# Gate rows and gated biases of the experts as single-pass products of 32 rows, issued at the end of a piece

## The chip, the cores and the metric

The kernel runs on one core of one Trainium2 chip. A core has a TensorE (matrix products into PSUM), a VectorE, a ScalarE, a GpSimd and a SyncE that issues the DMAs; in the profile they are PE (with PEld for its weight loads), DVE, ACT, POOL and SP. The metric is the device time of one execution in microseconds; the median of the runs counts.

## The reference

The input x is 8 images of 256 channels and 32 x 32 points. Layer 0 is a convolution and attention block. Layer 1 takes the 1024 points of an image as tokens t of 256 channels, adds a causal attention of the normalised tokens, and then adds a mixture of eight experts. Cut to what matters here:

```python
def ffn(x, Wr, br, W1, ..., W2, ..., Wo, bo):      # x: normalised tokens (b, f, d)
    feat = mean(x, axis=0)                         # over the images
    w = softmax(feat @ Wr + br, axis=-1)           # (f, e): one gate per token place and expert
    h = relu(bn(einsum('bfd,edh->bfeh', x, W1) + b1))
    h = relu(bn(einsum('bfeh,ehk->bfek', h, W2) + b2))
    y = einsum('bfeh,ehd->bfed', h, Wo) + bo
    return einsum('bfed,fe->bfd', y, w)
```

All eight experts are computed for every token; the gate only weights them. The gate depends on the place f and the expert e, not on the image. So the weighted biases, the sum over e of w[f,e] * bo[e], are the same for all images too.

## The kernel before

The kernel works in three parts. Layer 0 (to about 1421 us) and the attention of layer 1 (to about 2085 us) are untouched but for their tail. The third part, the experts, runs from about 2090 us to the end.

**Gates.** The function `gate(h)` handles one half h of the 1024 places. TensorE forms the logits lg (matmuls with feat as weights), VectorE and ScalarE make a softmax in `ge` (128 places x 4 tiles x 8 experts), four transposes turn it into PSUM (`pwT`, 8 x 512), and VectorE copies it to `wT` (8 experts x 1024 places, f32). `gate(0)` runs in the last stretch of the attention, ahead of the layer norm of the last half; `gate(1)` is the last work before the experts.

**Visits and pieces.** The experts are taken in two groups G of four. A visit is (G, half h, image b), 32 in all, in the order G, then h, then b; each has four slots s, one per expert: 128 pieces. Piece n starts layer 1 (W1) of its own expert, while layer 2 (W2) works on piece n-2 and layer 3 (Wo) on piece n-4. In the loop over n, four rounds i = 0..3 advance the three layers as generators and then do the VectorE and ScalarE steps that were put off from the piece before (`soon`). The engines are driven through `InOrder`, which keeps the program's order on each of them, so what is written first is queued first.

**Precision.** Most expert products are F32R, in one pass, of 12-bit upper and lower parts (`products`); layer 2 of the even experts is plain f32 (`pm<-h,w`). The gate rows and the gated biases are plain f32.

**Gate rows.** `gate_rows(G, h, s)` spreads the gate of one expert over all 128 partitions: a product of `sel8` (8 x 8 x 128, ones where row and expert agree) with `wT`, into `pw`, and a ScalarE copy to `wb`. Layer 2 multiplies by it (`gated`) three pieces later. It is needed only for the first image of a (G, h), so at 16 pieces: 0 to 3, 32 to 35, 64 to 67 and 96 to 99. `gated_bias(h, g)` does the same with `boT` (the expert biases, transposed on TensorE through `pbo`), into `pg` and then `gb`, for pieces 0, 1, 32 and 33. `gb` is added to the tokens `te` at slot 2. Both are issued at the head of the piece, before layer 1.

**Buffers.** PSUM has eight banks: one each for the two outputs of layer 1 (`pa`), two for `pm`, `pw`, `pg` and `pbo` together (pool `ps_b`), and four for layer 3 (`q`). Two products in a row for the same bank have to wait for whoever reads it.

**Queues.** SyncE issues all DMAs in order. At the opening of the experts it issues the remaining weights, the tokens `te` and the parts `ze` of the next visits, about 10 MB.

**Opening.** The tiles of the experts (pool `hp`) take over memory of the attention's pools, so the first instruction of each engine on such a tile waits until the attention's last users are done. `sel8` is made there by GpSimd (a memset, line 1626, and an affine select, line 1627).

The calls in the loop, which the change moves:

```python
if b == 0:
    gate_rows(G, h, s)
    if G == 0 and s < KC:
        gated_bias(h, s)
```

Of the kernel before, what the change touches and what calls it, by code (L numbers as in the profile page):

```python
# [9 lines left out]
F32 = mybir.dt.float32  # L10
F32R = mybir.dt.float32r
AF = mybir.ActivationFunctionType
ALU = mybir.AluOpType
# [4 lines left out]
P = 128  # L18
B, C, H, W = 8, 256, 32, 32
N = H * W  # L20
HALF = 512
KC = C // P
NH, KD, HD = 4, 32, 64
HID = 2 * C
NE = 8
# [79 lines left out]
def conv_attn_hybrid_kernel(  # L105
# [22 lines left out]
    nc = tc.nc  # L128
# [11 lines left out]
    def col(name, i=0, n=1):  # L140
        o, w = _VOFF[name]
        assert i + n <= w
        if o >= NVEC0:
            return more[0][:, o - NVEC0 + i : o - NVEC0 + i + n]
        return vec[:, o + i : o + i + n]

    def cols(name):
        return col(name, 0, _VOFF[name][1])

    ident = const.tile([P, P], F32, name="ident")  # L150
# [323 lines left out]
    pe, dve = InOrder(tc, nc.tensor, TensorCost()), InOrder(tc, nc.vector, vector_cost)  # L474
    act, pool = InOrder(tc, nc.scalar), InOrder(tc, nc.gpsimd)
    t = [None] * B
    with ExitStack() as l0:
        wpool = l0.enter_context(tc.tile_pool(name="w0", bufs=1))
        one = l0.enter_context(tc.tile_pool(name="one0", bufs=1))
# [27 lines left out]
        sel = one.tile([nf, P], F32, tag="full", name="sel", bufs=2)  # L507
# [60 lines left out]
        for half in range(2):  # L568
            nc.gpsimd.affine_select(
                out=pickr, in_=pickr, compare_op=ALU.not_equal, fill=1.0, base=-NH * half,  # L570
                pattern=[[-1, NH], [0, HD]], channel_multiplier=1,
# [7 lines left out]
        for half in range(2):  # L579
            nc.gpsimd.affine_select(  # L580
                out=pickn, in_=pickn, compare_op=ALU.not_equal, fill=1.0, base=-nq * half,
                pattern=[[-1, nq]], channel_multiplier=1,
# [444 lines left out]
        def gate(b):  # L1027
            hid = hid_of[b]
            while len(hid["out"]) < hid["gelu"] and ng + len(hid["out"]) in hid["h"]:
                g = len(hid["out"])  # L1030

                prod = two.tile([P, N], F32, tag="hid", name="hid", bufs=ng + 1)
                blocks = prod.rearrange("p (n k r c) -> p k n r c", r=PS, k=2, c=W // 2)
                a, b2 = (hid["h"][j].rearrange("p (n r k c) -> p k n r c", r=PS, k=2, c=W // 2) for j in (g, ng + g))
                for k in range(2):
                    dve.tensor_mul(blocks[:, k], a[:, k], b2[:, k])
                hid["out"].append(prod)
                if hid["alone"]:
                    mix(b, g)
# [189 lines left out]
    wm = ctx.enter_context(tc.tile_pool(name="wm", bufs=1))  # L1229
# [3 lines left out]
    nc.sync.dma_start(wrs, wr.rearrange("(k p) e -> p k e", p=P))  # L1233
    brs = wm.tile([1, NE], F32, name="brs")
    nc.sync.dma_start(brs, br)
    wT = wm.tile([NE, N], F32, name="wT")

    NG, SLOTS = 2, NE // 2
    w_d = [[dram.tile([P, 3, KC, C], F32, tag=f"wd{e}_{l}", name=f"wd{e}_{l}") for l in range(3)] for e in range(NE)]
# [2 lines left out]
    def in_parts(e, l):  # L1242

        return l != 1 or e % 2 == 1

    def load_expert(pool_, e, l):

        tag = f"w{e % SLOTS}_{l}"
        if not in_parts(e, l):
            w_ = pool_.tile([P, KC, C], F32, tag=tag, name=tag, bufs=1)  # L1250
            nc.sync.dma_start(w_, w2[e].rearrange("(k p) o -> p k o", p=P))
        else:
            w_ = pool_.tile([P, 3, KC, C], F32R, tag=tag, name=tag, bufs=1)
            nc.sync.dma_start(w_.bitcast(F32), w_d[e][l])
        w_in[e, l] = w_

    def upper(dst, src, eng=None, positive=False):

        if eng is None:
            act.activation(dst[:, 0], src, AF.Relu if positive else AF.Copy, scale=DOWN)  # L1260
        else:
            eng.tensor_scalar_mul(dst[:, 0], src, DOWN)
# [13 lines left out]
    with ExitStack() as l1:  # L1276
        wpool = l1.enter_context(tc.tile_pool(name="w1", bufs=1))
        one = l1.enter_context(tc.tile_pool(name="one1", bufs=1))
# [3 lines left out]
        ps_t = l1.enter_context(tc.tile_pool(name="ps_t1", bufs=2, space=PSUM))  # L1282
# [10 lines left out]
        def load_w(name, src):  # L1293
# [12 lines left out]
            out=lower, in_=lower, compare_op=ALU.is_ge, fill=0.0, base=0, pattern=[[-1, P]], channel_multiplier=1,  # L1306
# [225 lines left out]
        def gate(h):  # L1532

            nt = NT // 2
            lg = ps_m.tile([P, nt, NE], F32, tag="mm", name="lg")
            for i in range(nt):
                c0 = (h * nt + i) * P
                for k in range(KC):
                    pe.matmul(lg[:, i, :], feat[:, k, c0 : c0 + P], wrs[:, k, :], start=(k == 0), stop=False)
                pe.matmul(lg[:, i, :], ones[0:1, :], brs, start=False, stop=True)  # L1540
            yield 2.0
            ge = one.tile([P, nt, NE], F32, tag="ge", name="ge")
            gs = one.tile([P, nt], F32, tag="gs", name="gs")
            dve.tensor_reduce(gs, lg, AX.X, ALU.max)
            dve.tensor_sub(ge, lg, gs.unsqueeze(2).to_broadcast([P, nt, NE]))
            act.activation(ge, ge, AF.Exp)
            yield 1.0
            dve.tensor_reduce(gs, ge, AX.X, ALU.add)
            dve.reciprocal(gs, gs)
            dve.tensor_mul(ge, ge, gs.unsqueeze(2).to_broadcast([P, nt, NE]))  # L1550
            yield 1.0
            pwT = ps_t.tile([NE, HALF], F32, tag="tp", name="pwT")
            for i in range(nt):
                pe.transpose(pwT[:, i * P : (i + 1) * P], ge[:, i, :], ident)
            dve.tensor_copy(wT[:, h * HALF : (h + 1) * HALF], pwT)
            yield 0.5

# [51 lines left out]
    with ExitStack() as l2:  # L1609
        hp = l2.enter_context(tc.tile_pool(name="hp", bufs=2))  # L1610
        ps_a = l2.enter_context(tc.tile_pool(name="ps_a2", bufs=2, space=PSUM))
        ps_b = l2.enter_context(tc.tile_pool(name="ps_b2", bufs=2, space=PSUM))
# [9 lines left out]
        s2b = const.tile([P, KC * NE], F32, name="s2b")  # L1622
        nc.vector.tensor_scalar_mul(s2b, s2, -1.0 / STEP)

        sel8 = hp.tile([NE, NE, P], F32, name="sel8", bufs=1)
        nc.gpsimd.memset(sel8, 0.0)
        nc.gpsimd.affine_select(
            out=sel8,
            in_=sel8,
            compare_op=ALU.not_equal,  # L1630
            fill=1.0,
            base=0,
            pattern=[[-1, NE], [0, P]],
            channel_multiplier=1,
        )

        boT = hp.tile([NE, KC, P], F32, name="boT", bufs=1)
        bo_g = cols("bo").rearrange("p (e g) -> p g e", g=KC)
        pb = ps_b.tile([NE, KC, P], F32, tag="pm", name="pbo")
        for g in range(KC):  # L1640
            pe.transpose(pb[:, g, :], bo_g[:, g, :], ident)
        dve.tensor_copy(boT, pb)

        visits = [(G, h, b) for G in range(NG) for h in range(2) for b in range(B)]
        pieces = [(v, s) for v in range(len(visits)) for s in range(SLOTS)]
        ts, gate_of, bias_of, h1_of, h2_of, acc_of = {}, {}, {}, {}, {}, {}

        def cut(h):
            return slice(h * HALF, (h + 1) * HALF)
# [13 lines left out]
        def gate_rows(G, h, s):  # L1663

            wb = gate_of[G, h, s] = hp.tile([P, HALF], F32, tag=f"wb{s}", name=f"wb{s}", bufs=1)
            pw = ps_b.tile([P, HALF], F32, tag="pm", name="pw")
            pe.matmul(pw, sel8[:, G * SLOTS + s, :], wT[:, cut(h)], start=True, stop=True)
            act.copy(wb, pw)

        def gated_bias(h, g):  # L1670

            if g == 0:
                bias_of[h] = hp.tile([P, KC, HALF], F32, tag="gb", name="gb", bufs=1)
            pw = ps_b.tile([P, HALF], F32, tag="pm", name="pg")
            pe.matmul(pw, boT[:, g, :], wT[:, cut(h)], start=True, stop=True)
            act.copy(bias_of[h][:, g, :], pw)
# [77 lines left out]
        def layer3(v, s):  # L1754
# [8 lines left out]
            for both in (False, True):  # L1763
                for g in range(KC):
# [12 lines left out]
                    yield  # L1777

        load_expert(hp, 1, 1)
        fetch_t(0)  # L1780
        for s in range(1, SLOTS):
# [5 lines left out]
        for n in range(len(pieces) + LAG3):  # L1787
            one_ = two_ = three = iter(())
            if n < len(pieces):
                v, s = pieces[n]  # L1790
                G, h, b = visits[v]
                if b == 0:
                    gate_rows(G, h, s)
                    if G == 0 and s < KC:
                        gated_bias(h, s)
                if s == 1:
                    fetch_t(v + 1)
                    if v >= 1:
                        fetch_z(v + 1)
                if s == 2 and G == 0:  # L1800
                    dve.tensor_add(ts[v], ts[v], bias_of[h])
                one_ = layer1(v, s)
            if 0 <= n - LAG2 < len(pieces):
                two_ = layer2(*pieces[n - LAG2])
            if n >= LAG3:
                three = layer3(*pieces[n - LAG3])

            now, soon = soon, [[] for _ in range(4)]
            for i in range(4):
                for stage in (one_, two_, three):  # L1810
                    next(stage, None)
                for step in now[i]:
                    step()
            for l, lag in enumerate((0, LAG2, LAG3)):
                if 0 <= n - lag < len(pieces):
                    v, s = pieces[n - lag]
                    if visits[v] == (0, 1, B - 1):
                        load_expert(wm if s == 0 or (s, l) == (1, 0) else hp, SLOTS + s, l)
# [114 lines left out]
```

## Time and profile before

| what | value |
|---|---|
| median of 3 runs | 3236.74 us (3234.16 to 3243.24) |
| the profiled execution | 3235.5 us, of which its span is 3233.8 us |
| TensorE busy | 2962.3 us, 92% of the span |
| VectorE, ScalarE, GpSimd busy | 2385.1, 1569.5, 337.9 us |
| mean granted TensorE clock | 0.964 |

The span is from the first to the last instruction. Busy time of TensorE counts matmuls whose ends are modelled. "PE pw" names the engine and the tile written; `pw<-wT,sel` names what is written and what is read, and the shapes after it give the partitions and elements. An arrow in brackets names what ended the idle time before an instruction. Nearly all instructions carry line 72, the helper that records them, so they are told apart by their tiles.

### The profile page before, as it was taken

The page shows a single profiled execution, that of the slowest core. Times are in us where ns is not written, and L with a number is a line of the kernel's source. Part 1 is how long each engine was busy: PE and PEld are TensorE (multiplying, and loading weights), DVE is VectorE, ACT ScalarE, POOL GpSimd, SP SyncE. Part 2 cuts the span into 40 slices and gives each one's busy share as a digit, 9 for nine tenths or more (in the row PEclk, how much of TensorE's full clock was granted, in tenths as well). Part 3 has the DMA queues.
Part 4 walks back from the last instruction along what each step waited for, and adds up shares of the span by engine and source line. Part 5 has one row for each costly group of instructions (what it writes and reads, how often), then busy time and mean ns, then how long its engine had stood idle before and what let it go on. Part 6 is the DMA issues. An engine that isn't in the chain of part 4 may idle for free.

```text
span 3233.8 us, 41619 instructions
## 1 busy us (share of the span) xinstructions
PE 2962.3 (92%) x16822; PEld 1941.5 (60%) x16822; DVE 2385.1 (74%) x3002; ACT 1569.5 (49%) x2312; POOL 337.9 (10%) x410
## 2 busy tenths in 40 slices
PE   5998899989898999859999999799999999999998
PEld 3654545454555555435666555577767777777776
DVE  1378778777877878655666655488878888887887
ACT  1554455545445445313333333266656666666665
POOL 1121111121212110001122222100000000000000
PEclk9999999999999999989999999799999999999999
DMA  4203030303030300011323311322211242221220
GB/s 149 62 19 79 27 79 27 79 27 79 27 79 27 79 14 8 17 71 69 142 112 118 124 79 52 136 111 86 78 66 66 92 139 103 91 72 65 84 80 26
DMA packets 60061, 237.46 MB, mean 73 GB/s; under 512 B 5382, under 2 KB 13654, under 8 KB 50774
## 3 DMA queue, kind: packets, MB, share of 16 engines
q1 hardware_dynamic: 59862, 234.74, 21.5%
q8 instruction: 134, 2.20, 0.3%
q14 instruction: 65, 0.53, 0.0%
HBM read 143.23 MB, written 91.49 MB: 73 GB/s over the span
## 4 chain that ended last, share of the span: by engine, by line
PE 45%; DVE 7%; ACT 2%; issue 1%; POOL 1%; DMA 0%; SPq 0%; POOLq 0%; ACTq 0%; DVEq 0%
PE pm L72 12%; PE pa L72 11%; PE q L72 11%; PE s L72 4%; PE po L72 3%; PE pv L72 2%; DVE nm L72 1%; DVE pr L72 1%; PE pk L72 1%; DVE parts L72 1%; DVE zt L72 1%; ACT pr L72 1%; DVE st L72 1%; PE tpt L72 1%; PE pw L72 1%
## 5 line engine op out<-in xcount | busy, mean ns | idle before, releaser
L72 PE MATMUL q<-h2p,w 128*128 128x512 f32 x1536 | 485.9, 425 | 2.9 <-DVE h2p L72 1.7
L72 PE MATMUL pa<-ze,w 128*128 128x512 f32 x1488 | 422.5, 392 | 0.0
L72 PEld LDWEIGHTS q<-h2p,w 128*128 128x128 f32 x1536 | 288.9, 188 | 118.2 <-issue 60.4
L72 DVE SCALAR_TENSOR_TENSOR x<-hpad,vec,x 128x1024 f32<-128x1024 f32 x248 | 317.1, 1283 | 39.9 <-ACT x L72 32.8
L72 DVE SCALAR_TENSOR_TENSOR conv<-hpad,vec,conv 128x1024 f32<-128x1024 f32 x256 | 329.3, 1293 | 13.8 <-ACT conv L72 7.2
L72 PEld LDWEIGHTS pa<-ze,w 128*128 128x128 f32 x1488 | 278.9, 188 | 69.8 <-issue 9.5
L72 ACT ACTIVATE h<-pa,bn_o,s1a 128x512 f32<-128x512 f32 x256 | 198.8, 777 | 203.4 <-PE pa L72 203.3
L72 ACT ACTIVATE pT<-s 128x1024 f32<-128x1024 f32 x256 | 247.4, 1024 | 69.1 <-PE s L72 69.1
L72 DVE SCALAR_TENSOR_TENSOR h<-pa,s1b,h 128x512 f32<-128x512 f32 x256 | 191.6, 749 | 113.2 <-PE pa L72 100.8
L72 PE MATMUL po<-pT,vT 128*32 128x256 f32 x4096 | 272.1, 383 | 0.0
L72 PE MATMUL ph<-xn,piw 128*128 128x512 f32 x512 | 244.4, 615 | 3.1 <-DVE xn L72 1.6
L72 PE MATMUL s<-kk,z 128*128 128x512 f32 x512 | 245.2, 609 | 0.9 <-DVE pr L72 0.9
L72 PE MATMUL pm<-h,w 128*128 128x512 f32 x512 | 242.0, 595 | 0.0
L72 PE MATMUL pm<-h1p,w 128*128 128x512 f32 x768 | 216.1, 389 | 0.5 <-DVE h1p L72 0.5
L72 DVE SCALAR_TENSOR_TENSOR o<-vpad,pe_w,o 128x1024 f32<-128x1024 f32 x128 | 163.5, 1282 | 45.2 <-ACT o L72 42.0
L72 PE MATMUL s<-qst,kst 128*128 128x256 f32 x1024 | 175.2, 313 | 14.2 <-DMA kst<-part 12.9
L72 ACT ACTIVATE hpad<-ph,pi_o 128x512 f32<-128x512 f32 x126 | 86.9, 690 | 182.4 <-PE ph L72 182.4
L72 ACT ACTIVATE h2p<-h 128x1024 fp32r<-128x1024 f32 x128 | 134.9, 1054 | 77.8 <-DVE h L72 77.8
L72 PEld LDWEIGHTS po<-pT,vT 128*32 128x32 f32 x4096 | 120.2, 110 | 84.5 <-issue 1.9
L72 PEld LDWEIGHTS s<-qst,kst 128*128 128x128 f32 x1024 | 136.8, 192 | 47.5 <-issue 42.4
L72 PEld LDWEIGHTS pm<-h1p,w 128*128 128x128 f32 x768 | 144.1, 188 | 31.5 <-DVE h1p L72 0.9
L72 PE MATMUL pz<-pow__116,hid 128*128 128x256 f32 x512 | 138.2, 426 | 27.1 <-DVE hid L72 27.1
(241 smaller groups left out, 4811.7 us busy)
## 6 DMA issues: line engine op xcount, KB each, us to landing
ze<-zd SPq DMA_DIRECT2D x31, 1536.0 KB, 6.3
zd<-parts SPq DMA_DIRECT2D x16, 1536.0 KB, 5.5
qst<-part SPq DMA_DIRECT2D x32, 512.0 KB, 8.5
kst<-part SPq DMA_DIRECT2D x32, 512.0 KB, 15.2
te<-ud SPq DMA_DIRECT2D x32, 512.0 KB, 3.9
wd<-parts_w SPq DMA_DIRECT2D x20, 768.0 KB, 3.6
w<-wd SPq DMA_DIRECT2D x20, 768.0 KB, 5.9
t<-in_x_dram SPq DMA_DIRECT2D x8, 1024.0 KB, 4.9
```

Of the source, the lines that this page charges most:

```text
L72: return self._tc.keep_in_program_order(method(*args, **kwargs))
```

## The change

The products of the gate rows and of the gated biases become F32R products over 32 rows: four parts times eight experts. A helper `stacked` splits its source in an upper part (a cast to F32R) and the rest, and lays four copies of the parts side by side in a given order. For the gates the order is upper, lower, upper, lower (`ge4`), for the biases upper, upper, lower, lower (`bo4`), so that the sum over 32 rows holds all four products of parts. For the gate rows `sel8` picks the first two parts alone (ones in rows e and 8 + e). The transposes give 32 rows in place of 8. `sel8` is built in another tile `sel`, which shares the place of `h1p`, by a memset and two selects, and cast by a fourth GpSimd instruction. Last, the calls move from the head of a piece to its end: after the four rounds, before the loads of the next group.

```diff
-    wT = wm.tile([NE, N], F32, name="wT")
+    wT = wm.tile([4 * NE, N], F32R, name="wT")
...
+    def stacked(dst, src, order):
+
+        first = [order.index(i) for i in range(2)]
+        dve.tensor_copy(dst[:, :, first[0]].bitcast(F32R), src)
+        dve.tensor_sub(dst[:, :, first[1]].bitcast(F32R), src, dst[:, :, first[0]])
+        for i, part in enumerate(order):
+            if i not in first:
+                dve.tensor_copy(dst[:, :, i], dst[:, :, first[part]])
...
+            ge4 = one.tile([P, nt, 4, NE], F32, tag="ge4", name="ge4")
+            stacked(ge4, ge, (0, 1, 0, 1))
             yield 1.0
-            pwT = ps_t.tile([NE, HALF], F32, tag="tp", name="pwT")
+            pwT = ps_t.tile([4 * NE, HALF], F32, tag="tp", name="pwT")
             for i in range(nt):
-                pe.transpose(pwT[:, i * P : (i + 1) * P], ge[:, i, :], ident)
+                pe.transpose(pwT[:, i * P : (i + 1) * P], ge4[:, i].rearrange("p a e -> p (a e)"), ident)
...
-        sel8 = hp.tile([NE, NE, P], F32, name="sel8", bufs=1)
-        nc.gpsimd.memset(sel8, 0.0)
-        nc.gpsimd.affine_select(
-            out=sel8,
-            in_=sel8,
...
+        sel8 = hp.tile([4 * NE, NE, P], F32R, name="sel8", bufs=1)
+        sel = hp.tile([4 * NE, NE, P], F32, tag="h1p", name="sel", bufs=1)
+        nc.gpsimd.memset(sel, 0.0)
+        for part in range(2):
+            nc.gpsimd.affine_select(
+                out=sel,
+                in_=sel,
...
+                base=-NE * part,
...
+        nc.gpsimd.tensor_copy(sel8, sel)
...
-        boT = hp.tile([NE, KC, P], F32, name="boT", bufs=1)
-        bo_g = cols("bo").rearrange("p (e g) -> p g e", g=KC)
-        pb = ps_b.tile([NE, KC, P], F32, tag="pm", name="pbo")
+        boT = hp.tile([4 * NE, KC, P], F32R, name="boT", bufs=1)
+        bo4 = hp.tile([P, KC, 4, NE], F32, name="bo4", bufs=1)
+        stacked(bo4, cols("bo").rearrange("p (e g) -> p g e", g=KC), (0, 0, 1, 1))
+        pb = ps_b.tile([4 * NE, KC, P], F32, tag="pm", name="pbo")
         for g in range(KC):
-            pe.transpose(pb[:, g, :], bo_g[:, g, :], ident)
+            pe.transpose(pb[:, g, :], bo4[:, g].rearrange("p a e -> p (a e)"), ident)
         dve.tensor_copy(boT, pb)
...
-                if b == 0:
-                    gate_rows(G, h, s)
-                    if G == 0 and s < KC:
-                        gated_bias(h, s)
...
+            if n < len(pieces) and b == 0:
+                gate_rows(G, h, s)
+                if G == 0 and s < KC:
+                    gated_bias(h, s)
```

## The prediction, made before the changed kernel was run

> **What bounds the kernel now.** I read the page first: busy shares and the costliest groups. TensorE is busy 92% of a span of 3233.8 us, against 74% for VectorE. The changed lines all lie after about 2070 us, where the experts run. Two groups of the page, and two of the by-form list for the products that the change rewrites:
>
> ```profile
> L72 PE MATMUL pa<-ze,w 128*128 128x512 f32 x1488 | 422.5, 392 | 0.0
> L72 PE MATMUL pm<-h1p,w 128*128 128x512 f32 x768 | 216.1, 389 | 0.5 <-DVE h1p L72 0.5
> L72 PE MATMUL pw<-wT,sel 8*128 8x512 f32 x32 | 18.9, 671 | 1.9 <-POOL sel L1627 1.9
> L72 PE MATMUL pg<-wT,boT 8*128 8x512 f32 x8 | 5.5, 766 | 0.7 <-ACT wb L72 0.7
> ```
>
> The last column is idle time before the group: next to none, so in the expert stage TensorE is the bound and time taken off it counts in full. The windows say the same, 240.00 us busy of 240.00 from 2680 to 2920. A gate row (pw) is 16 products in 32 records: two records each, so more than one pass.
>
> Second, the PE timeline at a gate row (first three lines) and at a boundary of pieces without one (last three); columns are start, length, instruction.
>
> ```profile
> 2645.93 0.61 PE L72 MATMUL q<-h2p,w 128*128 128x512 f32 x2
> 2646.47 1.12 PE L72 MATMUL pw<-wT,sel 8*128 8x512 f32 x2
> 2648.56 1.02 PE L72 MATMUL pm<-h,w 128*128 128x512 f32 x2
> ...
> 2129.89 0.62 PE L72 MATMUL q<-h2p,w 128*128 128x512 f32 x2
> 2130.35 1.09 PE L72 MATMUL pa<-ze,w 128*128 128x512 f32 x4
> 2131.28 1.07 PE L72 MATMUL pm<-h1p,w 128*128 128x512 f32 x4
> ```
>
> From q to pm is 2.63 us with the row and 1.39 us without (both hold two q and four pa): a row costs 1.24 us.
>
> Third, the chain of waits where the stage opens.
>
> ```profile
> 2089.54 1.02 PE pwT L72 x4
> 2090.69 0.92 POOL sel L1626
> 2091.65 1.14 POOLq L1929
> 2092.84 2.07 PE pw L72 x2
> 2094.91 1.71 PE pg L72 x2
> 2096.62 2.86 PE pa L72 x6
> 2099.49 2.31 PE pa L72 x6
> 2101.80 1.05 PE pw L72 x2
> ```
>
> The first row waits for GpSimd to build sel8, and runs at half clock (2.07 against 1.05 us): TensorE is at 0.50 until about 2101.0 by short windows. The first real work, pa, starts at 2096.6.
>
> Fourth, piece 32, the first of half 1, in the PE timeline and the windows (start:end, length, busy PE, PEld, DVE, ACT, POOL, clock):
>
> ```profile
> 2361.35 1.12 PE L72 MATMUL pw<-wT,sel 8*128 8x512 f32 x2
> 2363.15 1.51 PE L72 MATMUL pg<-wT,boT 8*128 8x512 f32 x2 [0.68 <-ACT wb L72]
> 2365.00:2370.00 5.00, 5.00 (x9) 2.55 (x9) 2.37 (x3) 1.06 (x2) 0.00 (x0) 0.50 0.49 187
> ```
>
> The bias product waits for the copy of the row before it, since the pool gave both one PSUM bank; after this sparse stretch the clock halves, from about 2363.8 to 2370.6. The windows from 2102 to 3200 show no other dip.
>
> **What the Trainium skill says.** "FP8 and Floating Point Precision", TensorE Precision Notes: true FP32 takes 4 passes. The trace agrees: four single-pass pa take 0.91 us in the chain (0.228 each), two f32 pm of the same size 1.72 us (0.86 each), a ratio of 3.8. "TensorE: Matmul & The Clock Gate", LDWEIGHTS: the load depends on columns, not rows. The trace agrees: 181 to 184 ns for 8x128, 188 for 128x128, so 32 rows should cost no more than 8. The same page, Part 1: the clock is set by free-running windows of about 3.4 us. The trace fits: the dip lasted 6.8 us, two windows, and the opening stayed cold 4.4 us after pa began.
>
> **The change, part by part.** The sum is against the profiled execution, 3235.5 us (span 3233.8 and 1.7 around it); the median of the runs is 3236.74, 1.2 above.
>
> *Rows in steady state* (12: pieces 32 to 35, 64 to 67, 96 to 99). Of 1.24 us, 0.86 is the four passes and 0.38 goes with going into a 32-row tile of the array and back, weights not loaded ahead. Single pass: 0.23 plus that 0.38, 0.61. Both tile sizes are unchanged in the built program. No trace line shows this exact form. Nearest are the layer-0 products rb (8 rows, single pass), two of 256 columns in 0.34 us, which lie between the bounds. Bounds: 0.23 (no overhead left, saves 1.01) and 0.61 (saves 0.63). I take 0.60, saving 0.65: 12 x 0.65 = 7.8.
>
> *Bias in steady state* (2). In piece 33 pg follows pw 0.95 us later; single pass about 0.3, saving 0.6. But in the built order pg of piece 33 now waits for VectorE's reading of the last pm. In the trace of before that reading ends at 2387.52, and pg would be ready about 2387.1: minus 0.45. Net 0.15. Piece 32: saving 0.6; the bank of pg is now one that ACT has long read, so the 0.7 stall goes. With 0.6 us of sparse work in place of 3.2, I expect the dip to go too, 6.8 us at half speed, 3.4. Together 4.7, bounds 1.3 (dip stays) and 4.7.
>
> *Opening.* Added on the path: four VectorE instructions in each gate (copy, subtract, two copies of 128x32). Nearest rows are 0.19 us at a pitch of 0.22; I take 0.85 for four, bounds 0.6 and 0.9. Gate 0 is exposed: pwT waits for it, tpt is queued behind pwT, and ACT and the layer norm behind tpt; minus 0.85. Gate 1 is exposed likewise. Then pbo, which waited for nothing, must wait for bo4: wT's copy 0.61 and four instructions 0.8 after pwT. So pa starts at 2089.54 + 0.85 + 1.05 + 0.61 + 0.8 + 0.06 + 0.45 (two pbo) = 2093.4 instead of 2096.6: 3.2 earlier with gate 1 inside. GpSimd now needs 0.94 + 2 x 1.1 for the selects + a cast of 1024, about 1.0 scaled from 387 ns for 256, + gaps: 4.5 us from 2091.5, so 2096; the first pw comes after twelve pa at half clock, 5.2 us, about 2098.5. Hidden, with 2.5 us to spare; uncovered it would cost its lateness.
> Then pieces 0 to 3. Before, twelve pa, pw and pg end at 2103.7; after, 2098.6 + 0.9 = 2099.5, the clock still partly cold: 4.1 ahead. The second pair is now at the end of piece 1 (0.9 in place of one row, 1.24): 0.3 more. Piece 2: 0.65 more. The fourth row, now at the end of piece 3, has no counterpart: minus 0.6. Net 4.4, less gate 0: 3.5. Bounds 2.0 and 5.5: the clock's window may open 1.7 us earlier or later, worth half of it.
> Moved past other queues: SP's DMAs keep their order; the first load of weights waits for pwT, 0.85 later. Those loads fill the queue until 2117 at about 400 GB/s; w of piece 2 lands near 2101 (needed 2104), z of visit 1 at 2112.9 + 0.9 (needed about 2116.5). Hidden, by 2 to 3 us.
> The add of gb in piece 2 now waits for a copy made at the end of piece 1 with h's VectorE steps queued behind it: about 0.2, inside the bounds. In piece 34 the trace has VectorE reach that add at 2388.65 and gb would be there at 2388.6: nothing.
> The ACT copies of wb move from the head of a piece to its end. ACT is idle 1.3 to 1.7 us before them in the trace, and next pa only needs ACT 0.9 us later: nothing.
>
> *Sum.* 7.8 + 0.15 + 4.7 + 3.5 = 16.1 us. 3235.5 - 16.1 = 3219.4, and 1.2 more for the median: 3220.6.
>
> **Rivals.** What this kernel's measurement tells from no change is 0.3%, 9.7 us: faster is below 3227.0, slower above 3246.5.
> *A, forecast*: 3220.6, own range 3215 to 3226.
> *B, the clock gives it back*: the dip of piece 32 is only where a free-running window happened to lie, and another comes elsewhere, or the opening stays cold a window longer. Gain 16.1 - 3.4 - 1.5 = 11.2, 3225.5. For: the three runs before already spread over 9 us. Against: the dip follows the only stretch of 3 us without full-height products.
> *C, no overhead stays on the small products*: 12 x 0.36 + 4 x 0.3 = 5.5 more, 3215. For: equal load times. Against: the load before pw and the one after it are both late in the trace (0.36 and 0.76 us).
> *D, slower*: at a piece's end the product waits for its PSUM bank, as pg did in piece 32, and pa queues behind it. At 0.68 us a time, 20 products lose 13.6 and the gain is nearly gone; slower takes (16.1 + 9.7)/20 = 1.3 us each; at 1.5 us the time is 3250. For: only two banks serve pm, pw and pg. Against: in the built order every pw waits for ACT alone, on readings that ACT has done in the trace, and only one pg waits for VectorE.
> VectorE as the new bound is excluded: 30 of 40 us busy in the pieces with rows.
>
> **How the numbers follow.** A 0.65, B 0.20, C 0.12, D 0.03. Faster: nearly all of A (0.62), half of B (0.10), C: 0.84. Slower: D, 0.03. Same: 0.13. The range must leave at most 0.2 out: 3212 holds C's middle, 3230 holds B with a further dip of 3.4.
>
> **What would show it.** pw and pg as one record each, 16 and 4; q to pm across a gate row 1.8 to 2.1 us instead of 2.63; pa's first start about 3 us after the last pwT, and no GpSimd step in the chain there; no clock below 1.00 around piece 32; pg of piece 33 with a short wait for VectorE. The prediction is wrong if pw still takes over 0.9 us of TensorE, if the rows wait for banks, or if early pieces wait for weights.

## The result, and the profile after

The changed kernel takes 3221.35 us (median of 6 runs, 3216.75 to 3228.38) beside 3240.11 us (6 runs, 3234.16 to 3246.16) for the kernel before: a ratio of 0.9942, 95% interval 0.9926 to 0.9958. A second measurement further below gives 0.9961 (0.9947 to 0.9975). It is faster, by 0.4 to 0.6%.

The profiled execution of the changed kernel took 3223.6 us with a span of 3221.4, the one of before 3235.5 with 3233.8. That difference of 12.4 us can't be read as the gain: the part of the program ahead of gate 0, which the change doesn't touch, was 4.19 us longer in the profile of after (gate 0's first product starts at 2063.05 before and at 2067.24 after; in a second profile of before it starts at 2067.99). From here on traces are compared from that product to the start of the last group of q products: 1161.60 us before, 1145.04 after, **16.56 us less**. To the end of the span it is 1170.75 and 1154.16, 16.6 less; some expectations below use that measure.

The groups by form of the changed kernel (name, tile, shape, count, then busy us and mean ns, then idle time before):

```profile
L72 PE MATMUL pw<-wT,sel 32*128 32x512 f32 x16 | 7.9, 494 | 0.0
L72 PE MATMUL pg<-wT,boT 32*128 32x512 f32 x4 | 1.7, 417 | 0.2 <-DVE h L72 0.2
```

One record for each product instead of two, and 9.6 us of TensorE where the two groups had 24.4. The same gate row as in the prediction, in the PE timeline (start, length, instruction):

```profile
2647.67 0.62 PE L72 MATMUL q<-h2p,w 128*128 128x512 f32 x2
2648.22 0.49 PE L72 MATMUL pw<-wT,sel 32*128 32x512 f32 x1
2648.64 1.19 PE L72 MATMUL pa<-ze,w 128*128 128x512 f32 x4
2649.67 1.08 PE L72 MATMUL pm<-h1p,w 128*128 128x512 f32 x4
...
2370.57 0.50 PE L72 MATMUL pw<-wT,sel 32*128 32x512 f32 x1
2370.91 0.39 PE L72 MATMUL pg<-wT,boT 32*128 32x512 f32 x1
2371.23 1.19 PE L72 MATMUL pa<-ze,w 128*128 128x512 f32 x4
...
2379.61 0.50 PE L72 MATMUL pw<-wT,sel 32*128 32x512 f32 x1
2380.35 0.50 PE L72 MATMUL pg<-wT,boT 32*128 32x512 f32 x1 [0.24 <-DVE h L72]
```

From q to pm is 2.00 us instead of 2.63. The middle part is piece 32: no wait between pw and pg, 0.66 us for both, where it was 3.24. The last part is piece 33: pg waits for VectorE and comes 0.74 us after pw instead of 0.34. Behind piece 32 the windows (start:end, length, busy PE, PEld, DVE, ACT, POOL, then clock) show no dip, that is no stretch at half clock:

```profile
2370.00:2375.00 5.00, 5.00 (x22) 3.60 (x21) 4.94 (x6) 3.44 (x7) 0.00 (x0) 1.00 0.29 100
2375.00:2380.00 5.00, 5.00 (x22) 3.74 (x20) 3.47 (x5) 2.93 (x4) 0.00 (x0) 1.00 0.00 0
```

The chain of waits where the stage opens looks different from the one expected:

```profile
2094.97 1.03 PE pwT L72 x4
...
2096.12 0.92 POOL sel L1638
...
2097.11 1.15 POOL sel L1640
2098.26 0.41 issue
2098.66 0.59 PE pbo L72 x2
2099.25 1.72 PE pa L72 x4
```

Two GpSimd steps of the selector stand between pwT and pbo, though pbo reads only what VectorE wrote; pa starts 4.28 us after pwT by this chain.

Where the 16.56 us lie (starts in us since gate 0's first product; first pa from the chain, the rest from the timeline):

| stretch | before | after | gained |
|---|---|---|---|
| to gate 1's pwT (two stacks of four VectorE steps) | 26.49 | 27.73 | -1.24 |
| to the first pa | 33.57 | 32.01 | 1.56 in all |
| to the first pa of piece 4 | 58.34 | 54.30 | 4.04 in all |
| from there to the last q | 1103.26 | 1090.74 | 12.52 |

### The profile page after: what moved, and what is told of

Its sections match the earlier page's. It is cut to its first block, busy times and chain, and to the rows that moved or that the text cites. A ratio compares the mean times of both kernels' runs of the same rounds, so it can differ in the third digit from the quotient of the medians.

```text
span 3221.4 us, 41596 instructions
## 1 busy us (share of the span) xinstructions
PE 2946.4 (91%) x16802; PEld 1937.0 (60%) x16802; DVE 2389.3 (74%) x3014; ACT 1567.9 (49%) x2312; POOL 338.3 (11%) x412
## 4 chain that ended last, share of the span: by engine, by line
PE 44%; DVE 7%; ACT 2%; issue 1%; POOL 1%; DMA 0%; SPq 0%; ACTq 0%; POOLq 0%; DVEq 0%
PE pm L72 12%; PE pa L72 11%; PE q L72 11%; PE s L72 3%; PE po L72 3%; PE pv L72 2%; DVE nm L72 1%; DVE pr L72 1%; PE pk L72 1%; DVE parts L72 1%; DVE zt L72 1%; ACT pr L72 1%; DVE st L72 1%; PE tpt L72 1%; PE tpz L72 1%
```

## Experiments

The theory has four parts. A row's saving is passes alone. The rest of a row (0.38 us) belongs to the change of tile. The move is worth the opening, the bank wait and the clock's dip. And GpSimd held up VectorE in the opening. The table has what all runs gave; "stretch" is gate 0's first product to the last q, from one profile each, and ratios are to the kernel before on the same chip.

| kernel | ratio of times (95%) | stretch, us |
|---|---|---|
| before / again | 1 | 1161.60 / 1159.89 |
| changed | 0.9942 (0.9926 to 0.9958) | 1145.04 |
| changed, again | 0.9961 (0.9947 to 0.9975) | 1145.13 |
| move only | 0.9985 (0.9977 to 0.9993) | 1153.42 |
| passes only | 0.9961 (0.9948 to 0.9974) | 1148.58 |
| rows twice | 0.9967 (0.9956 to 0.9978) | 1148.53 |
| 128 rows | 0.9935 (0.9922 to 0.9949) | 1139.60 |
| GpSimd later | 0.9957 (0.9948 to 0.9966) | 1144.44 |
| 128 rows, bias transposes late | 0.9932 (0.9917 to 0.9947) | 1137.68 |
| the same, again | 0.9934 (0.9920 to 0.9947) | 1138.38 |
| 20 products of 32 rows at three places | one run each, no ratio | 1162.76 |
| 20 products of 128 rows at three places | one run each, no ratio | 1152.69 |
| 4 f32 products of 8 rows at three places | one run each, no ratio | 1173.43 |

### One part of the change at a time

The kernel before with the move alone:

```diff
-                if b == 0:
-                    gate_rows(G, h, s)
-                    if G == 0 and s < KC:
-                        gated_bias(h, s)
...
                 for step in now[i]:
                     step()
+            if n < len(pieces) and b == 0:
+                gate_rows(G, h, s)
+                if G == 0 and s < KC:
+                    gated_bias(h, s)
```

> The kernel before with one part of the change alone: the calls of gate rows and gated bias stand at the end of the piece; the products keep 8 rows, f32 and four passes. Measure: from gate 0's first product to the end of the span (1170.75 us before, 1154.16 after), and the clock round piece 32. Theory S (products of 8 of 128 rows count as hardly any activity for the clock, and bring the dip of piece 32): 2.6 us of such products still stand together, so a dip remains; q to pm across a steady row stays 2.63; gained are the wait of pg for its bank (0.7) and the opening, where pa no longer stands behind GpSimd (2.2) and behind products at half clock (about 1): 4 us. Rival I (the idle 0.7 us of pg's wait brings the dip): no dip, 7.4 us gained.

The changed kernel with these calls where they were before:

```diff
                 G, h, b = visits[v]
+                if b == 0:
+                    gate_rows(G, h, s)
+                    if G == 0 and s < KC:
+                        gated_bias(h, s)
...
-            if n < len(pieces) and b == 0:
-                gate_rows(G, h, s)
-                if G == 0 and s < KC:
-                    gated_bias(h, s)
```

> The changed kernel with its calls back at the head of the piece: single-pass products of 32 rows, not moved. Theory S: no dip at piece 32 (3.4 us gained), steady rows save 12 x 0.65 = 7.8, rows of pieces 1 to 3 about 2; the opening now waits for all four GpSimd steps (about 4 us lost) and for two stacks (1.3 lost), while its products cost about 2.8 less: together some 10 us gained, 1161, and piece 32 keeps the 0.7 wait of pg for its bank. Rival I: the idle 0.7 us brings the dip all the same: 6.5 us gained, 1164. If moving and passes were independent, the gains of this kernel and of the one with the move alone would add up to 16.6.

The move alone gained 8.2 us (to the end of the span 1162.55): 4.12 up to piece 4, as much as the whole change, and 4.06 after it, as much as the bank wait (0.7) and the dip (3.4) together. The times give it less: a ratio of 0.9985 is 4.9 us, with an interval from 2.3 to 7.5. The passes alone gained 13.0 (to the end of the span 1157.65, against the 1161 and 1164 expected; the opening, where the expectation's terms add up to a loss of about 0.5, gained 1.86). Neither shows a dip at piece 32. Their PE timelines and windows there, first the move alone,

```profile
2371.81 1.12 PE L72 MATMUL pw<-wT,sel 8*128 8x512 f32 x2
2372.77 1.02 PE L72 MATMUL pg<-wT,boT 8*128 8x512 f32 x2
2373.72 1.19 PE L72 MATMUL pa<-ze,w 128*128 128x512 f32 x4
...
2370.00:2380.00 10.00, 10.00 (x40) 6.88 (x39) 8.50 (x9) 6.00 (x9) 0.00 (x0) 1.00 0.19 54
```

then the passes alone:

```profile
2365.49 0.50 PE L72 MATMUL pw<-wT,sel 32*128 32x512 f32 x1
2366.66 0.50 PE L72 MATMUL pg<-wT,boT 32*128 32x512 f32 x1 [0.68 <-ACT wb L72]
2367.09 1.19 PE L72 MATMUL pa<-ze,w 128*128 128x512 f32 x4
...
2366.00:2376.00 10.00, 9.34 (x33) 6.13 (x33) 9.74 (x12) 6.18 (x8) 0.00 (x0) 1.00 0.64 247
```

The first has the f32 products without the wait, 1.91 us from pw to pa; the second the wait without the f32 products, 1.60 us; the kernel before had both, 3.24 us. Rival I (the wait suffices) fell with the second kernel, which has the wait and no dip. Theory S as written (the low products, those of 8 or 32 rows, bring the dip by themselves) fell with the first, though its stretch was shorter than the 2.6 us expected. What is left is the length of the whole stretch. The two gains add to 21.2 and not to 16.6, mostly because each removes the dip by itself and so each is credited with its 3.4 us; the opening, too, is gained by either (4.12 and 1.86, against 4.04 together).

In the kernel with the passes alone pw waits for all of GpSimd's selector (its first pw 5.58 us after pwT starts), which is what the move hides. Near the end of the program it had a dip of its own, of one window: its windows from 3206 to 3210 show the clock at 0.69 and 0.50, which is worth up to 1.7 us.

### Does the dip belong to the program?

The kernel before, profiled again.

> The kernel before once more, for its trace alone. Theory S+I (the dip of piece 32 comes of the sparse products and the 0.7 us wait together): a stretch at 0.50 again at piece 32, at the same place in the program. Rival R (the clock's windows run free of the program, and the stretch is only caught by chance): no dip this time, or one of another length; from gate 0's first product to the last q 1158.2 instead of 1161.6.

Its windows (start:end, length, busy times, clock):

```profile
2368.40:2368.80 0.40, 0.40 (x2) 0.00 (x0) 0.37 (x1) 0.00 (x0) 0.00 (x0) 0.99 1.08 461
2369.20:2371.60 2.40, 2.40 (x6) 1.82 (x6) 2.40 (x3) 0.68 (x2) 0.00 (x0) 0.50 0.77 320
2372.00:2372.40 0.40, 0.40 (x2) 0.24 (x1) 0.30 (x1) 0.29 (x1) 0.00 (x0) 0.74 1.05 410
```

The dip is there again, right behind pw and pg, but 3.4 us long instead of 6.8. Theory S+I named its place and rival R its length. It cost 3.4 us in one profile and 1.7 in the other, which is the difference of their stretches. Measured against this profile the move alone gained 6.5 us and the changed kernel 14.8.

To see what makes a dip, three kernels repeat the product of pieces 32, 64 and 96 back to back: 20 times in the changed kernel, 20 times in the kernel with 128 rows (its edit is in the next part), and 4 times as f32 products of 8 rows in the kernel before:

```diff
-            pe.matmul(pw, sel8[:, G * SLOTS + s, :], wT[:, cut(h)], start=True, stop=True)
+            for _ in range(20 if s == 0 and (G, h) != (0, 0) else 1):
+                pe.matmul(pw, sel8[:, G * SLOTS + s, :], wT[:, cut(h)], start=True, stop=True)
```

> The changed kernel with the gate row's product of three pieces (32, 64 and 96) computed 20 times over: 5.2 us of single-pass products of 32 rows without a gap at three places. Theory S (a stretch of low products as long as about one window of 3.4 us halves the clock, without any idle time): a stretch at 0.50 right after each of the three, 3.4 or 6.8 us long. Rival I (idle time is needed): no clock below 1.00 there; the three places cost 19 x 0.24 = 4.6 us each and nothing more.

> The kernel with 128 rows, with the same three products computed 20 times over: the array is loaded over its full height, but 96 of the rows are zeros. Theory S, if the tile's height is what counts: no clock below 1.00, each place costs 19 x 0.23 = 4.3 us. If the data's zeros count as no activity: stretches at 0.50 as with 32 rows.

> The kernel before with the gate row's f32 product of pieces 32, 64 and 96 computed four times over: 3.6 us of products of 8 rows, at piece 32 followed by the bias product's wait and product as before. Theory S: a stretch at 0.50 after each of the three. Rival I: one after piece 32 only, where the wait of 0.7 us stands.

PE timeline at piece 32 and the windows behind it, 32 rows:

```profile
2373.05 4.82 PE L72 MATMUL pw<-wT,sel 32*128 32x512 f32 x20
2378.03 2.07 PE L72 MATMUL pa<-ze,w 128*128 128x512 f32 x4
...
2378.00:2380.00 2.00, 2.00 (x6) 1.58 (x6) 0.00 (x0) 0.99 (x2) 0.00 (x0) 0.50 0.00 0
```

and 128 rows:

```profile
2369.51 4.72 PE L72 MATMUL pw<-wT,sel 128*128 128x512 f32 x20
2374.29 1.07 PE L72 MATMUL pa<-ze,w 128*128 128x512 f32 x4
...
2374.00:2376.00 2.00, 2.00 (x10) 1.65 (x10) 0.00 (x0) 1.62 (x3) 0.00 (x0) 1.00 0.00 0
```

With 32 rows four pa take 2.07 us and the clock is at 0.50, in all three places for about 3.4 us, while TensorE had no idle time. With 128 rows the same number of products takes nearly the same time and leaves the clock at 1.00 in all three. Beside the same kernel without the repeats, the stretch grew by 13.1 us with 128 rows, three times 19 x 0.23, and by 17.7 with 32 rows; the dips make most of the difference. With 8 rows in f32 there are three dips, 6.8 us long at piece 64, where no wait stands beside the products:

```profile
2652.34 4.26 PE L72 MATMUL pw<-wT,sel 8*128 8x512 f32 x8
...
2656.00:2662.00 6.00, 6.00 (x10) 3.02 (x10) 2.36 (x3) 1.36 (x2) 0.00 (x0) 0.50 1.01 349
```

Rival I falls: no idle time is needed. The length that theory S named, about one window, was too much. In each of these traces the clock's changes lie whole multiples of 3.41 us apart, so the time can be cut into windows of that length, and each dip starts at a window's end. In the first profile of before, pw starts at 2361.35 and the dip at 2363.75: 2.4 us of that window were low products and the wait between them. In the second profile it was 2.5 us, and at the six places with repeated products 2.4 to 3.4. Behind windows at full clock with 2.06 us of them or less it stayed at 1.00; the move alone had 1.5 us in one window, the passes alone 1.6. The dip went on for a second window where the first one at half clock still held 0.83 us or more of low products, and ended after one where it held 0.60 or less. So the program brings the dip, and how its products fall on the windows sets the length.

At the same length it is the height of the tile that counts, not the data, since 96 of the 128 rows were zeros. The Trainium skill ("TensorE: Matmul & The Clock Gate", Part 1) has free-running windows of about 3.4 us, which agrees with dips of one or two times 3.4. It says that the clock follows how busy TensorE has been; here TensorE was busy without a gap with 32 rows and with 128, and only with 32 did the clock halve, so busy time alone does not decide.

### What a row costs

Each gate row's product twice, back to back:

```diff
             pe.matmul(pw, sel8[:, G * SLOTS + s, :], wT[:, cut(h)], start=True, stop=True)
+            pe.matmul(pw, sel8[:, G * SLOTS + s, :], wT[:, cut(h)], start=True, stop=True)
```

> The changed kernel with each of the 16 gate rows' products computed twice into the same place, back to back. Theory T (of a row's 0.61 us, 0.23 is the pass and 0.38 belongs to going into the 32-row tile of TensorE and back): the second one costs 0.23 to 0.25, q to pm across a steady row 2.24, 3.7 us over all. Rival O (every product of this form costs 0.61, its weights never being loaded ahead): q to pm 2.6, 9.8 us over all.

The operands filled up to 128 rows with zeros (likewise pwT, sel, boT, bo4 and pbo):

```diff
-    wT = wm.tile([4 * NE, N], F32R, name="wT")
+    wT = wm.tile([P, N], F32R, name="wT")
...
-            ge4 = one.tile([P, nt, 4, NE], F32, tag="ge4", name="ge4")
+            ge4 = two.tile([P, nt, P // NE, NE], F32, tag="wv", name="ge4", bufs=1)
+            pool.memset(ge4[:, :, 4:], 0.0)
...
-        sel8 = hp.tile([4 * NE, NE, P], F32R, name="sel8", bufs=1)
+        sel8 = hp.tile([P, NE, P], F32R, name="sel8", bufs=1)
```

> The changed kernel with gates, selector and biases filled up with zero rows to 128, so that the products are 128x128 as their neighbours are; same passes, same places, same VectorE and GpSimd steps but for memsets. Theory T: without a change of tile a row costs 0.23 instead of 0.61, q to pm across a steady row 1.62; 16 rows save 6.1 us and the bias products perhaps 0.5: 1147.5 instead of 1154.2, about 3214.5 in the runs. Rival O (the 0.38 comes of the order or of waits, not of the tile): no difference, 1154.

The steady row in the PE timeline, rows twice:

```profile
2649.40 0.62 PE L72 MATMUL q<-h2p,w 128*128 128x512 f32 x2
2649.95 0.73 PE L72 MATMUL pw<-wT,sel 32*128 32x512 f32 x2
2651.64 1.08 PE L72 MATMUL pm<-h1p,w 128*128 128x512 f32 x4
```

and with 128 rows:

```profile
2644.66 0.62 PE L72 MATMUL q<-h2p,w 128*128 128x512 f32 x2
2645.12 0.40 PE L72 MATMUL pw<-wT,sel 128*128 128x512 f32 x1
2646.27 1.07 PE L72 MATMUL pm<-h1p,w 128*128 128x512 f32 x4
```

From q to pm: 2.24 us with two products, so the second one costs 0.24; 1.61 with 128 rows, so a row costs 0.22 there and 0.61 in the changed kernel. Both are theory T's numbers: 0.23 for the pass and 0.38 for going into the 32-row tile and back. The weight loads (PEld) show it too. In the changed kernel the load of pw starts at 2648.22, together with its product and after 0.36 us without a load, and that of the next pa at 2648.64, again together with its product. With 128 rows the load of pw starts at 2644.89, 0.23 us ahead of its product. The Trainium skill ("TensorEngine Tiling (Array Packing)", Key Properties) says that a change of tiling mode drains TensorE; it gives no price, and these traces put it at 0.38 to 0.39 us for a visit. Whether TensorE drains or only the loads are held back they don't tell. The stretch with 128 rows is 5.44 us shorter than that of the changed kernel (6.6 expected), of which 4.82 lie after piece 4: twelve rows of 0.39 make 4.7. The opening gave only 0.62.

### What held the opening

```diff
+        nc.gpsimd.tensor_copy(sel[:, 0, : 2 * NE], bo4[: 4 * NE, 1, 2:].rearrange("p a e -> p (a e)"))
         nc.gpsimd.memset(sel, 0.0)
```

with bo4's four steps issued ahead of it.

> The changed kernel with one edge added: GpSimd begins the selector only after bo4 is finished (its first step copies a piece of bo4). VectorE's four steps for bo4 are the same. Theory P (VectorE's small copies of bo4 are held up by GpSimd's selects running at the same time): the two last copies take 0.3 us together as they did for the gates, not 1.16; bo4 is finished some 0.9 us sooner, first pa 3.1 to 3.4 us after the start of pwT instead of 4.3. Rival Q (these copies are slow by their own shape, 128x16 with gaps): they take 1.2 us again, pa starts at 4.3. The selector is later by about 1.2 us, ready about when the first pw wants it: a wait of up to 0.5 us there.

VectorE's steps for bo4 and GpSimd's beside them in the timeline, changed kernel:

```profile
2096.09 0.94 POOL L1638 MEMSET sel<- 32x1024 f32 x1 [13.73 <-PE pwT L72]
2096.62 0.44 DVE L72 CAST bo<-vec 128x16 fp32r<-128x16 f32 x1
2097.10 0.18 DVE L72 TENSOR_TENSOR bo<-vec,bo 128x16 fp32r<-128x16 f32 x1
2097.11 2.29 POOL L1640 TENSOR_SCALAR_AFFINE_SELECT sel<-sel 32x1024 f32<-32x1024 f32 x2
2097.19 1.16 DVE L72 COPY bo<-bo 128x16 f32<-128x16 f32 x2
```

and with GpSimd later:

```profile
2107.90 0.15 DVE L72 CAST bo<-vec 128x16 fp32r<-128x16 f32 x1
2108.09 0.17 DVE L72 TENSOR_TENSOR bo<-vec,bo 128x16 fp32r<-128x16 f32 x1
2108.18 0.29 DVE L72 COPY bo<-bo 128x16 f32<-128x16 f32 x2
```

Its chain of waits has no GpSimd step any more:

```profile
2106.24 1.02 PE pwT L72 x4
2107.27 1.51 issue
2108.78 0.59 PE pbo L72 x2
2109.37 1.72 PE pa L72 x4
```

Theory P holds: the same instructions take 0.15 and 0.29 us instead of 0.44 and 1.16. In the changed kernel the cast ends at 2097.06, as the memset ends (2097.03), and the first copy, which took 1.08 us of the 1.16, ends at 2098.27, as the first select does (2098.26). The Trainium skill ("SBUF — State Buffer", Who interferes with whom) says that VectorE's copies and casts can take a port pair that GpSimd shares, that the pair is locked for a whole instruction, and that the other engine waits for it entirely; both ends agree with that. pa starts 3.1 us after pwT, and the first pw does not wait for the later selector. But the stretch is only 0.6 us shorter: by short windows the clock came up 4.8 us after the first pa here and 2.5 us after it in the changed kernel (4.3 in the kernel before). The first twelve pa took 5.65 us here and 4.71 in the changed kernel, so 0.94 of the 1.58 us won at the start went on running longer at half clock.

### A version that is faster than both kernels

With 128 rows, and the transposes of bo4 and the copy to boT taken out of pa's way:

```diff
-        pb = ps_b.tile([P, KC, P], F32, tag="pm", name="pbo")
-        for g in range(KC):
-            pe.transpose(pb[:, g, :], bo4[:, g].rearrange("p a e -> p (a e)"), ident)
-        dve.tensor_copy(boT, pb)
...
             if n < len(pieces) and b == 0:
+                if n == 0:
+                    pb = ps_b.tile([P, KC, P], F32, tag="pm", name="pbo")
+                    for g in range(KC):
+                        pe.transpose(pb[:, g, :], bo4[:, g].rearrange("p a e -> p (a e)"), ident)
+                    dve.tensor_copy(boT, pb)
                 gate_rows(G, h, s)
```

> The kernel with 128 rows, and with the two transposes of bo4 and the copy to boT at the end of the first piece instead of ahead of it. Theory: pa then waits for pwT alone and starts 1.1 us after pwT starts instead of 4.2; piece 4 begins 2 to 3 us sooner, less what the clock's start takes back (0 to 1): 1137.5 from gate 0's first product to the last q against 1139.6 with 128 rows alone. Rival: the weights of pieces 1 and 2, still on their way, or the selector, not ready before 5.5 us after pwT, take the gain back: 1139.6, with new waits for DMA or GpSimd.

```profile
2091.30 4.92 PE L72 MATMUL pa<-z_first,w 128*128 128x512 f32 x12
2096.52 0.50 PE L72 MATMUL pw<-wT,sel 128*128 128x512 f32 x1
2097.75 0.50 PE L72 MATMUL pg<-wT,boT 128*128 128x512 f32 x1 [0.73 <-DVE boT L72]
```

In this timeline pa follows pwT (2090.56) at once, and pg now waits for boT, 0.73 us. The stretch is 1.9 us shorter than with 128 rows alone, close to the 2.1 expected, and 1.2 shorter in a second profile. What the rival named came too: a pa of piece 2 waits for weights still on their way, 0.17 us in the first profile and 0.78 in the second. In the times this kernel can't be told from 128 rows alone (0.9932 and 0.9934 beside 0.9935). Timed once more, side by side with the changed kernel:

> The changed kernel itself once more, beside the kernel with 128 rows and late bias transposes on the same chip. Theory: 0.994 to 0.995 of the kernel before, as in the first measurement, and no clock below 1.00 at piece 32.

> 128 rows and late bias transposes once more. Theory, from the traces (7.4 us less from gate 0's first product to the last q): 0.0023 below the ratio of the changed kernel in the same batch, 0.992. Rival: the gain of the traces is taken back where the whole program is timed, and both ratios are the same.

The changed kernel took 3224.39 us (5 runs, 3222.03 to 3228.38), this one 3216.79 (3209.99 to 3219.91), the kernel before 3237.49. The runs of the two don't overlap, the ratios (0.9961 and 0.9934) differ by 0.0027 where 0.0023 was expected, and the traces say 6.75 us. Both ratios are higher than expected (0.994 to 0.995, and 0.992). Their two intervals meet at 0.9947, so the ratios alone would leave it open; runs and traces together speak for the gain being real.

## Why the prediction was right

Its mechanism was right in the main: fewer passes on every row, no bank wait and no dip at piece 32, an earlier start of the opening; one step of the opening failed. That the sum came so close is in part luck: it was 16.1 us, and the traces have 16.56 against the first profile of before and 14.8 against the second. By its own steps:

- **Steady rows**: 12 x 0.65 = 7.8 was said; 12 x 0.63 = 7.6 measured. The split of 1.24 us into four passes and 0.38 for the tile was an inference from two numbers; the doubled rows and the 128 rows show it. The bound of 0.23, rival C, fell for the changed kernel; it is what 128 rows reach.
- **Bias and piece 32**: 0.15 and 4.7 were said; 12.52 less the rows' 7.56 leaves 4.96. The bank wait went, and pg of piece 33 waits as said (0.40 late, 0.45 said). The dip went, but its worth is no constant: 3.4 us in one profile of before, 1.7 in the other. The sum took the larger, the only one then on record.
- **Opening**: 3.5 was said, 4.04 measured, by two misses that nearly cancel. The stacks cost 0.6 each instead of 0.85. The step "0.8 for four" failed: bo4 took 1.73 us, from 2096.62 to 2098.35, since GpSimd held VectorE up; and with it the sign "no GpSimd step in the chain there" failed. So pa started 4.28 us after pwT, not 3.0, and was 1.56 ahead of before where 2.35 was said. The clock made about 0.5 us of this good: it came up 2.5 us after the first pa instead of 4.3, and the first twelve pa took 4.71 us where the sum had 5.2. The first pw and pg took 0.66 where it had 0.9.
- **Rival B** (the clock gives it back) has a true core: dips of one window do come by chance at the program's end, in the kernels with the passes alone and with GpSimd later and in the second profile of before. They move a run by 1 to 2 us: from the last q to the end of the span it is 10.2 us in the second profile of before and 10.7 with GpSimd later, where the first profile of before and the changed kernel have 9.1. They don't fall on one kernel.
- **Rival D**: no pw waits for a bank, and one pg waits 0.24 us.
- **The time**: 3220.6 against 3221.35 is closer than this measurement tells. The median of before moved from 3236.74 to 3240.11 with three more runs, and the two ratios of the changed kernel stand for 18.8 and 13.1 us. The 16.6 of the traces lies between.

## What to carry to other kernels

A small product between large ones is priced by three things: its passes, the visit to another tile size, and, if several fill most of one window of 3.4 us (2.4 us of it did, 2.1 did not), a clock that halves behind them. Filling its operands with zero rows to the neighbours' height cost no pass here and took away the last two. Where GpSimd fills a table beside small VectorE copies, price those copies by GpSimd's instructions, or keep what reads them off the path.

## What the runs showed that was not expected

- Products of 32 or 8 rows halve the clock while TensorE is busy without a gap (three places of three with 20 products of 32 rows, 4.8 us); 128 rows, 96 of them zero, do not (none of three).
- The dip starts at the end of a window of 3.41 us of which 2.4 us or more went to low products; 2.06 us or less left the clock at 1.00. The waits between such products are counted in.
- A visit to a 32-row tile costs 0.38 us for one product or two, and 20 in a row cost 4.82 us, 0.24 each.
- Two VectorE copies of 128x16 took 1.16 us beside a GpSimd select, and 0.29 without it.
- An opening started 1.6 us sooner was worth 0.6 us, since the clock came up 4.8 us after the first large product instead of 2.5.
